# Finishing the last but one projection's second half inside attention, and moving a small norm product to another tile and other PSUM banks

## The chip, the cores and the metric

The kernel runs on one core of a Trainium2 chip. A core has five engines that run side by side[...]: TensorE (PE in the profile, with its weight loads as PEld), VectorE (DVE), ScalarE (ACT), GpSimd (POOL) and SyncE (SP), which in this kernel issues every DMA. The metric is the time of one execution on the device in microseconds (us); a comparison takes the median of several runs. Lower is better.

## The reference, cut to what matters

The input x is 1024 tokens by 512 features. It is normalised, and two branches read it: an attention with 32 query heads and 8 key/value heads of 128 channels, and a feed-forward network with integer weights. The result is x plus the attention's output times a SiLU of the network's output.

```python
xn = layernorm(x)
q = rmsnorm((xn @ Wq.T) per head, q_norm_w)          # 32 heads of 128
k = rmsnorm((xn @ Wk.T) per head, k_norm_w)          # 8 heads
v = (xn @ Wv.T) per head
scores = q @ k.T / sqrt(128) + alibi bias, causal
attn = softmax(scores) @ v
s = attn @ Wo.T
g = silu(down(silu(xn @ gate) * (xn @ up)))          # weights dequantised by groups
out = x + s * g
```

All inputs and the output are float32. The kernel keeps that accuracy by splitting each operand of a product into a high and a low float16 part and adding three products (helper `mm3`, lines 112 to 116).

## The kernel before, in words

**Three stages.** First the feed-forward network (to about 217 us in the profile), then twelve projections (to about 493 us), then attention with the output product (to the end). The order of the instructions of every engine is written out by hand: an engine executes its instructions in the order in which the program issues them.

**The projections.** They are numbered k = 0 to 11 and run in the order kv0, q0, q1, kv1, q2, q3, kv2, q4, q5, kv3, q6, q7 (`projections`, lines 666 to 669). A q projection makes four query heads (512 columns), a kv projection two key heads and two value heads. Number 10 is q6, the last but one, and 11 is q7. Each runs over eight tiles t of 128 tokens (the loop at line 1088). A tile is twelve products of 512 columns into one PSUM bank (`Projection.tile`, line 570). ACT copies the bank to the float32 tile `f` (line 580) and sums its squares per head (line 582); for kv, ACT and DVE also split the values (lines 594 and 595). There are two PSUM rings of two banks for this: even tiles take "m", odd tiles "o". A tile can start when the bank of its ring's last but one user has been read.

**Preparing the next projection's weights.** While projection k runs, `prepare(k + 1, t)` (line 671) is called ahead of tile t. `squares` sums the squares of the weights on ACT (called at t = 6 of the projection before). `norms` (line 514) adds them over the partitions by a small product with ones on PE, and DVE makes a power of two per head from it (`am`, line 526 and those after). `split_head` (line 556) then splits a head's weights into `wh` on ACT (line 561) and `wl` on DVE (line 562), one head per tile. Where the small product lies in PSUM is told by `spare` (line 486): in the "m" ring, so as one more user between two even tiles.

**Finishing a half.** After tiles 3 and 7, `queue_half` (line 767) queues the finishing of four tiles: the inverse root (`inverse` on DVE, `newton` on POOL), and per tile a multiplication on POOL (`normalize`, line 636), a float16 split on DVE (`halves`, lines 648 and 649), a transpose by DMA (`transposed`, line 657) and a store to DRAM (`store`, line 662), each a step or two after the other. Each work is put in a list under the step at which it is due, `finish_step` (line 477) carries out what is due and advances the clock. There are three `f` tiles.

**Attention.** 256 steps n of 128 queries of one head. Eight groups of 32 steps, one per key/value head; a group has four query blocks of 256 tokens, named qb 0 to 3, whose work grows with qb. The first group takes them as 3, 2, 1, 0, later ones as 2, 3, 0, 1. At step n PE makes the scores of n (line 866, PSUM ring "s", two tiles of two banks), DVE adds the bias and takes the row's minimum for n - 1 (line 878), ACT takes the exponential (line 879), ACT and DVE split it into float16 parts (lines 898 and 907), SP transposes it by DMA (line 915), and five steps later PE multiplies by the values (line 930). The first eight steps are run within projections 10 and 11, one after every second tile (lines 1104 to 1106). Queries are written to DRAM per group and read back a block ahead of use; group 6 reads q6, group 7 takes q7 from SBUF.

**The last projection is finished late.** For q7, `queue_half` takes the steps from two tables: `LAST_ROOTS` (the roots of its two halves) and `LAST_PAIRS` (the step of `halves` for each tile). Its steps count from TILES = 96, the number of projection tiles. q6 has been finished at once, its second half within projection 11.

Of the kernel before, what the change touches and what calls it, by code (L numbers as in the profile page):

```python
# [29 lines left out]
NI = FF // P  # L30
# [22 lines left out]
VALUES_STEP = 24  # L53


LAST_ROOTS = {1: 24, 0: 36}
LAST_PAIRS = {4: 46, 5: 78, 6: 110, 7: 142, 2: 174, 3: 221, 0: 224, 1: 229}
LAST_QUERIES = {4: 217, 5: 219, 6: 225, 7: 227, 2: 233, 3: 235, 0: 241, 1: 243}

WO_SPLIT = 6  # L60
# [16 lines left out]
def attention_gated_by_ffn_kernel(ctx, tc, x, gu_w, gu_z, gu_s, dn_w, dn_z, dn_s, wq, wkv, wo, qnw, knw, out):  # L77
# [7 lines left out]
    def ps2(name):  # L85
        return psum[0].tile([P, 2, 512], F32, tag="s", name=name)

    def ps1(tag, name):
        return psum[0].tile([P, 512], F32, tag=tag, name=name)
# [22 lines left out]
    def mm3(ps, lhs, rhs, first, last):  # L112
        (lh, ll), (rh, rl) = lhs, rhs
        te.matmul(ps, lhsT=lh, rhs=rh, start=first, stop=False)  # L114
        te.matmul(ps, lhsT=lh, rhs=rl, start=False, stop=False)  # L115
        te.matmul(ps, lhsT=ll, rhs=rh, start=False, stop=last)  # L116
# [43 lines left out]
    def pair(name):  # L160
        return fpsum.tile([P, 2, 512], F32, tag="pair", name=name)
# [72 lines left out]
    def gu_total(unit, m):  # L234
        a = gu_sums[unit, m, 0]
        ge.tensor_tensor(a, a, gu_sums.pop((unit, m, 2)), ALU.add)
# [11 lines left out]
    def gu_finish(k):  # L248

        if behind[k]:  # L250
            (gu_gate, gu_h)[k](behind[k].pop(0))
# [166 lines left out]
    def dn_load(it):  # L418
        if it % 2 == 0:
            wi = gp.tile([P, 2, DM], I32, tag="wi", name=f"dni{it}", bufs=3)  # L420
            sp.dma_start(wi, dn_w[it * P : (it + 2) * P, :].rearrange("(t p) c -> p t c", p=P))
            dn_raw["pair"] = (wi, wi.bitcast(F32))
        zi = gp.tile([P, DM], I32, tag="dzi", name=f"dnz{it}")
        si = gp.tile([P, DM], F32, tag="dsi", name=f"dns{it}")
        sp.dma_start(zi, dn_z[it].partition_broadcast(P))
        sp.dma_start(si, dn_s[it].partition_broadcast(P))
        dn_raw[it] = tuple(w[:, it % 2, :] for w in dn_raw["pair"]) + (zi, si)

    def dn_dequant(it, engine=ge):
        wi, wf, zi, si = dn_raw[it]  # L430
        ve.tensor_tensor(wf, wi, zi, ALU.subtract)
        engine.tensor_tensor(wf, wf, si, ALU.mult)

    def dn_split_w(it):
        if it % 2 == 0:
            wh = gp.tile([P, 2, DM], F32R, tag="wq", name=f"dnh{it}", bufs=3)
            wl = gp.tile([P, 2, DM], F32R, tag="dwl", name=f"dnl{it}")
            dn_w_hl["pair"] = (wh, wl)
        dn_w_hl[it] = tuple(w[:, it % 2, :] for w in dn_w_hl["pair"])
        split_r(dn_raw.pop(it)[1], *dn_w_hl[it])  # L440

    def dn_split_h(it, tb):
        hh = gp.tile([P, 512], F32R, tag="hh", name=f"hh{it}_{tb}", bufs=3)
        hl = gp.tile([P, 512], F32R, tag="hl", name=f"hl{it}_{tb}", bufs=3)
        split_r(h[:, it, tb * 512 : tb * 512 + 512], hh, hl)
        dn_h_hl[it, tb] = (hh, hl)
# [3 lines left out]
    def wo_squares_load(g):  # L450
        wo_raw[g] = gp.tile([P, NH, DM], F32, tag=("gs", "us")[g % 2], name=f"wo_sq{g}")
        sp.dma_start(wo_raw[g], wo[g * NH * HD : (g + 1) * NH * HD, :].rearrange("(i p) c -> p i c", p=P))

    def wo_squares(g):
        w = wo_raw.pop(g).rearrange("p i c -> p (i c)")
        se.activation(w, w, AF.Square, accum_out=swo[:, g : g + 1])
# [6 lines left out]
    def norm_weights():  # L463
        sp.dma_start(qwb, qnw.partition_broadcast(P))
        sp.dma_start(kwb, knw.partition_broadcast(P))
        ve.tensor_tensor(wn, qwb, kwb, ALU.mult)
        ve.tensor_reduce(wm, wn, AX.X, ALU.max, apply_absolute_value=True)
        ve.tensor_scalar(wm, wm, 1e-5, None, ALU.max)
        for i in range(NH):
            ve.tensor_scalar(cs[:, i : i + 1], wm, STEEPER[i] / (Q_SCALE * Q_SCALE * math.sqrt(HD)), None, ALU.mult)  # L470
        ve.reciprocal(rc, cs[:, NH - 1 : NH])
        ve.reciprocal(wm, wm)
        ve.tensor_scalar(wn, wn, wm, -Q_SCALE, ALU.mult, ALU.mult)
# [10 lines left out]
        finishing.setdefault(clock[0] + steps, []).append(f)  # L484

    def spare(k, name):
        return ps1("m", name) if k else pair(name)[:, 0, :]

    class Projection:
        def __init__(self, k, kind, i):  # L490
# [175 lines left out]
    projections = []  # L666
# [4 lines left out]
    def prepare(k, t):  # L671

        if k < len(projections):
            p = projections[k]
            if t == -1:
                p.squares()
            elif t == 1:
                p.norms()
            elif t == 2:
                p.scale()  # L680
            elif t == 6:
                p.factors()
            if 2 <= t < 2 + p.n:
                p.split_head(t - 2)
            elif p.kind == "kv" and 4 <= t < 6:
                p.split_values(t - 4)

    def down_begin():
        dn_split_w(0)
# [4 lines left out]
    for it in range(3, NI):  # L694
        if it < 3 + 2 * KT:
            projections[(it - 3) // KT].load((it - 3) % KT)
        last = it == NI - 1
        gu_unit(
            it,
            None,  # L700
            it + 1 if not last else None,
            meanwhile={NI - 2: lambda: dn_dequant(0, ve), NI - 1: down_begin}.get(it, lambda: None),
            total=not last,
        )
        if it == NI - 5:
            prepare(0, -1)
        if it == NI - 4:
            prepare(0, 1)
        if it == NI - 3:
            dn_load(0)  # L710
            dn_load(1)
        if last:
            dn_load(2)
            dn_split_h(0, 1)
# [3 lines left out]
    for it in range(NI):  # L718
        for tb in range(2):
            if it == 0:  # L720
                two = [pair(f"dn_ps{tb}_{i}") for i in range(2)]
                acc[tb] = [two[i // 2][:, i % 2, :] for i in range(4)]
            if tb == 0:
                if it + 2 < NI:
                    dn_dequant(it + 2)
                if it + 3 < NI:
                    dn_load(it + 3)
                if it + 1 < NI:
                    dn_split_w(it + 1)
            if it + 1 < NI:  # L730
                dn_split_h(it + 1, tb)
            wh, wl = dn_w_hl[it]
            hh, hl = dn_h_hl.pop((it, tb))
            for i in range(4):
                c = slice(i * P, i * P + P)
                mm3(acc[tb][i], (hh[:, c], hl[:, c]), (wh, wl), it == 0, it == NI - 1)
            if tb:
                if 0 <= it - 3 < HKV:
                    wo_squares_load(it - 3)
                if 0 <= it - 5 < HKV:  # L740
                    wo_squares(it - 5)
                if it in (1, 2):
                    gu_total((NI - 1, None), it - 1)
                elif it == 3:
                    gu_finish(0)
                elif it == 4:
                    gu_finish(1)
                elif it == 5:
                    norm_weights()
                elif NI - 6 <= it < NI - 1:  # L750
                    prepare(0, 8 - NI + it)
                if it == NI - 2:
                    prepare(1, -1)
            if it == NI - 1:
                for i in range(4):
                    go = h[:, i, tb * 512 : tb * 512 + 512]
                    se.activation(go, acc[tb][i], AF.Silu)
                    sp.dma_start(gd[tb * 4 + i], go)
# [8 lines left out]
    def queue_half(p, half):  # L767

        last = p is projections[-1]

        def due(steps, i, f):
            if last and i is None:
                c = TILES + LAST_ROOTS[half]
            elif last:
                c = TILES + LAST_PAIRS[half * HT + i] - 4
            else:
                c = clock[0] + (i or 0)
            finishing.setdefault(c + steps, []).append(f)

        due(0, None, lambda: p.inverse(half))  # L780
        if p.by_root:
            due(1, None, lambda: p.newton(half, True))
        else:
            for i in range(3):
                due((i + 1) // 2, None, lambda i=i: p.newton(half, i == 0))
        for i in range(HT):
            t = half * HT + i
            due(4, i, lambda t=t: p.halves(t))
            due(2, i, lambda t=t: p.normalize(t))
# [221 lines left out]
    late, y_ = [], []  # L1011
    TILES = NT * len(projections)
# [140 lines left out]
```

## Time and profile before

| | us |
|---|---|
| median of 3 runs | 1066.66 (1065.36 to 1067.37) |
| the profiled execution, its own time | 1066.42 |
| its span in the trace | 1064.6 |
| PE busy | 1002.7 (94%) |
| DVE busy | 886.1 (83%) |
| ACT busy | 802.7 (75%) |
| POOL busy | 413.9 (39%) |
| packets of the DMA queue that SP issues to, share of 16 engines' span | 85.4% |

The profile is of one execution. A group of instructions is told by the line of the kernel, the engine and the names of what it writes and reads (out<-in). "Idle before" is the time that the engine stood still ahead of the instruction, and after the arrow stands what ended it. The ends of PE's products are modelled: a product of 512 columns is shown with 0.38 us, while one starts every 0.216 us. So PE is "busy" through short waits, and a loss on PE is best measured from start to start.

### The profile page before, as it was taken

The numbers are of one execution on the slowest core, as the hardware profiler recorded it, in microseconds if no ns is written. First come the engines' busy times: TensorE is split into PE (matmuls) and PEld (weight loads), VectorE is DVE, ScalarE is ACT, GpSimd is POOL, SyncE is SP. The second block draws the span as 40 slices with busy tenths as digits, with TensorE's granted clock in tenths as the row PEclk, the third lists the DMA queues.
The fourth block names the chain that finished last, engine by engine and source line by source line (L and its number), as shares of the span: only waits on it lengthen the run. The fifth ranks groups of instructions, "written<-read, shape, count | busy, mean of one in ns | idle before, by whom it ended". The sixth has DMA issues, their size and how long they took to land.

```text
span 1064.6 us, 18405 instructions
## 1 busy us (share of the span) xinstructions
PE 1002.7 (94%) x5913; PEld 584.6 (55%) x5913; DVE 886.1 (83%) x1745; ACT 802.7 (75%) x2160; POOL 413.9 (39%) x407
## 2 busy tenths in 40 slices
PE   7899899999989999898799999999999999999986
PEld 4344377844444444344566666566666666665563
DVE  7888996638778687788799899898998998979986
ACT  5777644778877787587778788797987888868862
POOL 2588653124545546361343215123141141250732
PEclk9999999999999999999999999999999999999998
DMA  6123259447988989989999999899999998999995
GB/s 202 49 100 119 70 170 302 166 139 162 219 228 188 242 203 235 279 179 207 226 193 214 195 200 222 167 227 197 189 207 193 197 223 182 221 224 194 231 189 129
DMA packets 455039, 204.39 MB, mean 192 GB/s; under 512 B 401506, under 2 KB 411038, under 8 KB 454942
## 3 DMA queue, kind: packets, MB, share of 16 engines
q1 hardware_dynamic: 454942, 203.21, 85.4%
q8 instruction: 46, 0.75, 0.3%
q14 instruction: 51, 0.42, 0.1%
HBM read 77.32 MB, written 27.27 MB: 98 GB/s over the span
## 4 chain that ended last, share of the span: by engine, by line
PE 48%; DVE 17%; ACT 13%; issue 10%; DMA 8%; SPq 2%; POOL 2%; DVEq 0%; ACTq 0%; POOLq 0%
PE gu_ps L267 6%; DMA pT<-p 4%; PE s L114 4%; DVE pf L878 3%; PE s L116 3%; PE s L115 3%; PE op L114 3%; PE op L115 3%; PE av L114 3%; PE op L116 3%; PE av L116 3%; PE av L115 3%; ACT p L898 2%; ACT pf L879 2%; PE ps_q L114 2%
## 5 line engine op out<-in xcount | busy, mean ns | idle before, releaser
L907 DVE SCALAR_TENSOR_TENSOR p<-pf,row,p 128x1024 f16<-128x1024 f32 (+7 forms) x256 | 227.8, 890 | 23.5 <-ACT p L898 20.3
L879 ACT ACTIVATE pf<-pf,row 128x1024 f32<-128x1024 f32 (+7 forms) x256 | 197.6, 772 | 57.2 <-DVE row L878 52.7
L878 DVE CUSTOM_DVE_ANT_0 pf<-s,trel,cs 128x1024 f32<-128x1024 f32 (+7 forms) x256 | 207.2, 809 | 13.7 <-PE s L116 13.4
L898 ACT ACTIVATE p<-pf,row 128x1024 f16<-128x1024 f32 (+7 forms) x256 | 196.5, 768 | 8.4 <-DMA pT<-p 3.5
L114 PE MATMUL av<-pT,vT 128*128 128x256 f16 (+1 forms) x640 | 167.8, 262 | 15.5 <-DMA pT<-p 15.5
L115 PE MATMUL av<-pT,vT 128*128 128x256 f16 (+1 forms) x640 | 167.8, 262 | 0.0
L116 PE MATMUL av<-pT,vT 128*128 128x256 f16 (+1 forms) x640 | 167.6, 262 | 0.0
L114 PE MATMUL s<-kT,qT 128*128 128x512 f16 (+3 forms) x384 | 125.0, 325 | 12.4 <-DVE row L878 12.1
L115 PE MATMUL s<-kT,qT 128*128 128x512 f16 (+3 forms) x384 | 125.0, 326 | 0.0
L116 PE MATMUL s<-kT,qT 128*128 128x512 f16 (+3 forms) x384 | 123.4, 326 | 0.0
L837 POOL TENSOR_SCALAR wor<-wor,rvs 128x512 f32<-128x512 f32 x32 | 54.5, 1702 | 162.8 <-DMA wor<-in_wo 141.5
L114 PE MATMUL ps_q<-wh_q,xth 128*128 128x512 f16 x256 | 97.6, 381 | 2.6 <-DVE am_q L526 2.5
L116 PE MATMUL ps_q<-wh_q,xtl 128*128 128x512 f16 x256 | 97.5, 381 | 0.0
L115 PE MATMUL ps_q<-wl_q,xth 128*128 128x512 f16 x256 | 97.5, 381 | 0.0
L114 PE MATMUL op<-woh,oh 128*128 128x512 f16 x248 | 94.5, 381 | 0.0
L115 PE MATMUL op<-wol,oh 128*128 128x512 f16 x248 | 94.3, 380 | 0.0
L116 PE MATMUL op<-woh,ol 128*128 128x512 f16 x248 | 94.2, 380 | 0.0
L114 PEld LDWEIGHTS <-vT 128*128 128x128 f16 x640 | 62.6, 98 | 56.6 <-DMA pT<-p 9.4
L115 PEld LDWEIGHTS <-vT 128*128 128x128 f16 x640 | 62.6, 98 | 41.3 <-issue 3.5
L941 ACT ACTIVATE oh<-av 128x256 f16<-128x256 f32 x128 | 47.7, 373 | 48.5 <-PE av L116 47.8
L636 POOL TENSOR_TENSOR f_q<-f_q,inv_q 128x512 f32<-128x512 f32 x64 | 77.4, 1237 | 1.1
L844 POOL TENSOR_TENSOR wol<-wor,woh 128x512 f16<-128x512 f32 x32 | 49.4, 1543 | 71.3 <-ACT woh L843 71.3
(194 smaller groups left out, 2255.6 us busy)
## 6 DMA issues: line engine op xcount, KB each, us to landing
qd<-tr_q SPq DMA_DIRECT2D x56, 256.0 KB, 3.4
qT<-qd SPq DMA_DIRECT2D x28, 512.0 KB, 4.5
wq<-in_wq SPq DMA_DIRECT2D x32, 256.0 KB, 3.9
wo_sq<-in_wo SPq DMA_DIRECT2D x8, 1024.0 KB, 9.1
wor<-in_wo SPq DMA_DIRECT2D x32, 256.0 KB, 3.7
gui<-in_gu_w SPq DMA_DIRECT2D x13, 512.0 KB, 3.5
wkv<-in_wkv SPq DMA_DIRECT2D x16, 256.0 KB, 3.8
vd<-v SPq DMA_DIRECT2D x8, 512.0 KB, 4.0
```

The lines of the kernel that those rows point to most:

```text
L114: te.matmul(ps, lhsT=lh, rhs=rh, start=first, stop=False)
L115: te.matmul(ps, lhsT=lh, rhs=rl, start=False, stop=False)
L116: te.matmul(ps, lhsT=ll, rhs=rh, start=False, stop=last)
L267: te.matmul(banks[j][:, k, :], lhsT=w[:, j, ws], rhs=x[:, j, k * 512 : k * 512 + 512], start=x is xth, stop=x is xtl)
L636: ge.tensor_tensor(f, f, ib, ALU.mult)
L837: ge.tensor_scalar(wor[g, i], wor[g, i], rvs[:, g : g + 1], None, ALU.mult)
L844: ge.tensor_tensor(wol[g, i], raw, woh[g, i], ALU.subtract)
L878: ve.tensor_tensor_reduce(p, ps, trel[g][:, S - w :], cs[:, hh : hh + 1], 3e38, ALU.add, ALU.min, least[:, c])
L879: se.activation(p, p, AF.Exp, bias=least[:, c], scale=-1.0, accum_out=total[:, c])
L898: se.activation(p16[u, qt][:, :, 0, :], pf[u, qt], AF.Copy, scale=scale[:, qt : qt + 1])
L907: ve.scalar_tensor_tensor(lo, p, scale, hi, ALU.mult, ALU.subtract)
L941: se.activation(oh, av_ps[u], AF.Copy, scale=1.0 / P_SCALE)
```

## The change

Three edits.

1. The second half of projection 10 (q6, tiles 4 to 7) is no longer finished within projection 11. Its root is due at step 28, its four `halves` at steps 36, 44, 52 and 60; `normalize` is due two steps before, the transpose one step after and the store three steps after each. q7's roots move from steps 24 and 36 to 66 and 70, and its first five `halves` from 46, 78, 110, 142, 174 to 76, 92, 108, 124, 140.
2. `norms` is called ahead of tile 2 instead of tile 1; with it `scale`, `factors`, `split_head` and `split_values` move by one tile. The fourth head's split is thus ahead of tile 6 instead of tile 5. For projection 0, which is prepared within the network, the calls are renumbered and nothing moves.
3. The small product of `norms` takes a tile of the scores' ring "s" for projections 1 to 10, and a bank of the ring "o" for projection 11, where it took one of "m".

```diff
-LAST_ROOTS = {1: 24, 0: 36}
-LAST_PAIRS = {4: 46, 5: 78, 6: 110, 7: 142, 2: 174, 3: 221, 0: 224, 1: 229}
+LAST_ROOTS = {1: 66, 0: 70}
+LAST_PAIRS = {4: 76, 5: 92, 6: 108, 7: 124, 2: 140, 3: 221, 0: 224, 1: 229}
+
+LATE_ROOTS = 28
+LATE_PAIRS = [36, 44, 52, 60]
...
     def spare(k, name):
-        return ps1("m", name) if k else pair(name)[:, 0, :]
+        if k == 0:
+            return pair(name)[:, 0, :]
+        return ps2(name)[:, 0, :] if k < len(projections) - 1 else ps1("o", name)
...
             if t == -1:
                 p.squares()
-            elif t == 1:
+            elif t == 2:
                 p.norms()
-            elif t == 2:
+            elif t == 3:
                 p.scale()
-            elif t == 6:
+            elif t == 7:
                 p.factors()
-            if 2 <= t < 2 + p.n:
-                p.split_head(t - 2)
-            elif p.kind == "kv" and 4 <= t < 6:
-                p.split_values(t - 4)
+            if 3 <= t < 3 + p.n:
+                p.split_head(t - 3)
+            elif p.kind == "kv" and 5 <= t < 7:
+                p.split_values(t - 5)
...
     def queue_half(p, half):
 
         last = p is projections[-1]
+        late = p is projections[-2] and half == 1
 
         def due(steps, i, f):
-            if last and i is None:
+            if late:
+                c = TILES + (LATE_ROOTS if i is None else LATE_PAIRS[i] - 4)
+            elif last and i is None:
                 c = TILES + LAST_ROOTS[half]
```

More of the change, by code (lines that the diff above doesn't have):

```diff
@@ L707, in attention_gated_by_ffn_kernel @@
         if it == NI - 4:
-            prepare(0, 1)
+            prepare(0, 2)
         if it == NI - 3:
@@ L750, in attention_gated_by_ffn_kernel @@
                 elif NI - 6 <= it < NI - 1:
-                    prepare(0, 8 - NI + it)
+                    prepare(0, 9 - NI + it)
                 if it == NI - 2:
```

## The prediction

> **What bounds the kernel now.** I first read the page: PE is busy for 94% of the span, DVE for 83%. So I went to the busy time by stretches (engine busy and number of instructions, granted clock, DMA share, GB/s), cut at the projections' end and at the blocks of attention's second group.
>
> ```profile
> 467.70:493.10 25.40, 24.24 (x120) 11.51 (x119) 20.66 (x32) 19.54 (x79) 11.82 (x17) 1.00 0.96 214
> 493.10:546.40 53.30, 43.85 (x339) 30.24 (x338) 42.82 (x102) 43.30 (x112) 17.84 (x25) 1.00 1.07 219
> 563.00:585.30 22.30, 21.56 (x148) 13.72 (x147) 21.97 (x37) 19.40 (x35) 8.96 (x6) 1.00 1.06 218
> 585.30:601.60 16.30, 15.34 (x125) 11.22 (x123) 12.55 (x35) 12.50 (x37) 5.57 (x7) 1.00 1.12 213
> 615.10:685.50 70.40, 68.38 (x481) 43.95 (x480) 63.15 (x139) 58.10 (x133) 18.51 (x15) 1.00 1.01 198
> ```
>
> PE (first busy column) sets the time almost everywhere: 68.4 of 70.4 us in the third group. It stands still mainly in two places. One is the start of attention, 493 to 546: 9.5 of 53.3 us. The other is inside the projections, where the timeline of PE shows it:
>
> ```profile
> 303.19 0.38 PE L116 MATMUL ps_q<-wh_q,xtl 128*128 128x512 f16 x1
> 305.03 0.17 PE L518 MATMUL n_ps<-sb_q,ones_bf 128*128 128x4 bf16 x1 [1.46 <-DVE v L595]
> ...
> 307.43 0.38 PE L116 MATMUL ps_q<-wh_q,xtl 128*128 128x512 f16 x1
> 309.05 0.38 PE L114 MATMUL ps_q<-wh_q,xth 128*128 128x512 f16 x1 [1.24 <-DVE am_q L526]
> ...
> 440.07 0.16 PE L518 MATMUL n_ps<-sb_q,ones_bf 128*128 128x4 bf16 x1 [2.71 <-DVE v L595]
> ...
> 440.50 0.63 PE L115 MATMUL ps_q<-wl_q,xth 128*128 128x512 f16 x1
> ```
>
> At projection 4's second tile the small product waits until DVE has read kv tile 6 out of the "m" bank it is to take; then tile 2 waits until DVE has read the small product. From start to start, less the pitch of 0.216: 305.03 - 303.19 - 0.22 = 1.62 and 309.05 - 307.43 - 0.22 = 1.40, so 3.03 us. Projection 7 repeats it (371.71 and 375.72, the same 1.46 and 1.24 of idle). At 440.07 (within projection 10) 2.87 us are lost, and the next seven products start every 0.42 instead of 0.216 us: another 1.3.
>
> For the start of attention I took the waits from 485 to 546, and SP's timeline:
>
> ```profile
> PE av L114 <- DMA pT<-p: 5.9, 5, 2.6
> PE s L114 <- DVE row L878: 4.7, 5, 1.8
> ```
>
> ```profile
> 489.49 1.29 SPq L657 DMA_TRANSPOSE tr_q<-q  x1
> 490.87 0.64 SPq L662 DMA_DIRECT2D qd<-tr_q  x1
> 491.60 1.37 SPq L657 DMA_TRANSPOSE tr_q<-q  x1
> 493.06 0.53 SPq L662 DMA_DIRECT2D qd<-tr_q  x1
> 493.65 3.63 SPq L915 DMA_TRANSPOSE pT<-p  x1
> 497.33 0.57 SPq L662 DMA_DIRECT2D qd<-tr_q  x1
> 498.08 1.59 SPq L915 DMA_TRANSPOSE pT<-p  x1
> ```
>
> The probabilities' transpose issued at 493.65 was ready on DVE at 490.15 (start plus length in DVE's timeline): SP was busy with q6's second half. Against DVE's ends, the next ones are issued 3.7, 2.6, 4.3, 5.6 and 6.2 us late, under 1 us only again from 541. In the third group the delay is mostly 0 to 0.8. So here SP and the DMAs behind it are late, and PE's products with the values wait for landings.
>
> **What the Trainium skill says.** "Perfetto Trace Analysis", section on the HWDGE DMA instruction: the shown length is the sequencer generating descriptors, and only at its end is it free for the next instruction; "What DMA-bound means" counts a solid sequencer track as a bound of its own. SP's rows above agree: one starts within 0.1 us of the last one's end. "DMA: Bandwidth & Descriptors", "Issuing engines are not separate DMA queues": all DMAs share 16 engines; the shares of 1.06 to 1.12 agree with crowding. "PSUM — Partial Sum Buffer", "Engine vs sequencer instructions": PE's products start in program order, so tile 1 cannot pass the waiting small product; the trace agrees. "TensorE: Matmul & The Clock Gate", Part 1: an idle window halves the clock; the doubled pitch after 440.07 fits, though the 1.6 us stops show none.
>
> **Part 1, the small product.** Nothing is added: the same 13 products and DVE operations, a tile later. In the "s" ring no bank is in use before step 0, so its wait goes, and even tiles then have both "m" banks. Who is late next? Tile 2 of projection 4 needs kv tile 6's bank: PE would reach it at 303.40 + 2.59 = 306.0, DVE's read ended at 304.97, margin 1.0 us. The fourth `wh` (0.75 us) now comes after kv tile 5's copies on ACT but still ahead of tile 6's, so their end doesn't move. Gain 3.03 twice, and 0.4 at projection 5's product; bound above 6.5, below 4 (if the margin goes half the time). I take 6.0. Cover for the later split: the fourth `wl` is needed only at the next projection, over a tile (2.6 us) later.
>
> Projection 10 differs. The product for 11 is now in "o" behind kv tile 7, read by DVE until 441.41; PE gets there at 437.2 + 2.6 = 439.8 and still waits 1.6, with tile 2 and step 1's scores queued behind it. Then DVE is the limit: it works from 439.6 to 463 with under 2 us idle. The fourth `wl` ended at 461.9; projection 11's first product began at 463.5. A tile later, it comes behind ACT's copies of tile 5 (1.5 us) and `wh` (0.7), at about 462.7. So PE gains 463.5 - 462.7 = 0.8, not 4.2. Bounds 0 and 4.2; I take 1.0.
>
> **Part 2, what leaves projection 11.** DVE loses four pairs (CAST 1.25, 1.26, 0.42, 0.42 and TENSOR_TENSOR 1.41, 0.69 three times: 6.8 us between 478.8 and 487.8) and a root (0.5); POOL 4.7 us and twelve small operations; SP four transposes and four stores (1.30 and 0.52 median: 7.3 us). DVE's scores of step 5 start at 484.4 though PE had them at 473.7. Without the pairs DVE and ACT are 4 to 7 us earlier with steps 5 to 8, and SP is free when they come. PE's loss from 485 to 546, from start to start, is 5.5 on DVE and 6.8 on landings: 12.3 is the bound above. Below: SP's first lateness, 3.5. The landings end PE's waits until 531.5 (slack 0.0 there), so PE gains what the transposes gain, 4 to 7; then SP again issues 16-block transposes of up to 3 us against steps of 2.1. I take 5.5.
>
> **Part 3, what arrives in the second group.** DVE: pairs at 36, 52 and 60 in addition (44 takes 46's place), 0.42 + 0.69 = 1.11 each; less one root (0.52), since q7's go to the third group. The blocks of qb 0 and 1 have 3.7 and 1.4 us of DVE idle for two of them; the first, in a block where DVE is idle 0.6 of 16.6, costs about 0.5. POOL: 1.3 each, covered (its waits there include 19.4 us for `trel`). SP: 1.82 per tile. Adding up SP's rows gives 21.3 us in the 22.3 from 563.0, 13.6 in the next 16.3. Pair 44 adds its transpose and store just there: 23.1 of 22.3. Behind them queue the transposes of the last qb 3 heads, which landed 1.5 and 0.1 us ahead of their products (589.1 and 599.0). So PE is held by about 2. Together 2.5; bound below 0.5 (another landing hides it), above 7.3 (all of SP's time on the path). Pairs 36, 52 and 60 find SP free for 2 to 6 us in their blocks.
>
> **Part 4, later groups.** Two roots enter qb 2 of the third group (1.0 of DVE in 0.3 idle), pairs at 92 and 124 fall into qb 1 with 1.4 idle, the sixth group loses its pair (up to 1.3 of PE's wait for DVE there). I take 0, bounds -1.5 and +1.5.
>
> **Sum.** 6.0 + 1.0 + 5.5 - 2.5 - 0 = 10.0 us. The profiled execution's span is 1064.6 and its own time 1066.42, 1.8 around it and 0.24 under the median. 1066.66 - 10.0 gives 1056.7; I say **1056.5**.
>
> **Rivals.**
> - *The second group gives most of the start back.* SP and the DMA share say that the work only moves from one crowded place to another. With 6 for SP and no gain in projection 10: 6.0 + 5.5 - 6 = 5.5, so 1061. Against it: SP has 8 us free over the other three blocks.
> - *The start is freed wholly.* Early probabilities and an empty SP remove most of the 12.3, and projection 10 gains 3: 6.5 + 3 + 9 - 2 = 16.5, so 1050. Against it: transposes of 3 us per 2.1 us step.
> - *Slower: stores block SP.* Each store of q6 waits on SP, two steps (4.2 us) after its transpose, for that to land. The landing took 3.6 median, 7.5 at most. If all four took 7.5, each would hold SP, and every transpose behind it, for 3.3; with 1.8 of issue, 4 x 5.1 = 20.4 against gains of 12.5: 1074. It decides when a tile costs over 3.1 us on PE's path. For it: nearly all slack at 589 and 599 is gone already. Against: two of the four lie in blocks with spare.
> - *The stops move rather than go.* ACT and DVE, at 18 of 21 us in q projections, become the limit, and PE stops elsewhere: parts 1 and 2 give 2.5, 1066.7. Against it: ACT itself waits 2.2 us for PE right after each stop (at 307.8).
>
> **How the numbers follow.** Chances: my forecast 0.54 (own range 1053 to 1060.5), second group gives back 0.22 (1059 to 1064), wholly freed 0.12 (1047 to 1053), slower by SP 0.07, stops move 0.05. The range from 1051 to 1063.5 takes in nearly all of the first two and a part of the third, 0.8 in all. About 0.2% (2.1 us) is what a measurement of this kernel can tell from no change. Faster: 0.54 + 0.22 + 0.12 = 0.88; within 0.2%: 0.05; slower 0.07.
>
> **What would show it.** Right: no idle ahead of the small product at projections 4 and 7, and none for `am`; at projection 11's first product a wait for `wl`; SP's transposes within 2 us of DVE from 490 to 510; a loss near the second group's qb 3 to qb 0 change behind q6's transposes. Wrong: the small product waiting for the squares instead, PE's stops in the first group unchanged, or a second group over 74 us (it took 68.7, from 546.4 to 615.1).

## The result and the profile after

The changed kernel takes 1072.57 us (median of 6 runs, 1071.88 to 1074.61) against 1067.70 for the kernel before (6 runs, 1065.36 to 1069.83): a ratio of 1.0049, interval 1.0032 to 1.0066. It is slower; 1056.5 was forecast. The profiled execution took 1072.69, its span is 1070.8, against 1064.6; these two lie 6.2 apart, the medians 4.9. Cut at ACT's copy of a projection's first tile and at DVE's first operation on the scores of a group, the spans differ like this (us):

| stretch | before | after | difference | forecast |
|---|---|---|---|---|
| network, to projection 0's first tile | 220.8 | 221.4 | +0.6 | 0 |
| projections 0 to 10 | 246.9 | 250.9 | +4.0 | -7.0 |
| projection 11 and first group | 78.7 | 72.8 | -5.9 | -5.5 |
| second group | 68.7 | 74.6 | +5.9 | +2.5 |
| third group | 70.4 | 72.8 | +2.4 | 0 |
| the rest | 379.1 | 378.4 | -0.7 | 0 |

One of the three large terms came out as forecast, the first group's. PE's waits in the projections, 223 to 493 us, in the changed kernel (line that waited, for whom, us in total, times, longest):

```profile
PE ps_q L117 <- ACT wh_q L566: 5.9, 3, 2.6
PE ps_q L118 <- DVE wl_q L567: 3.7, 3, 1.3
```

In the kernel before, the same stretch held these:

```profile
PE n_ps L518 <- DVE v L595: 5.6, 3, 2.7
PE ps_q L114 <- DVE am_q L526: 2.5, 2, 1.2
PE s L114 <- DVE row L878: 1.2, 2, 0.8
PE n_ps L518 <- ACT jk_q L582: 0.3, 1, 0.3
PE ps_kv L114 <- DVE v L595: 0.3, 1, 0.3
```

The waits at the small product are all gone, as forecast, and 9.6 us of waiting stand at another place where there were 9.9. The new place is the first tile of projections 4, 7 and 10. PE's timeline after, at projection 4:

```profile
302.51 0.38 PE L117 MATMUL ps_q<-wh_q,xth 128*128 128x512 f16 x1 [1.43 <-ACT wh_q L566]
304.14 0.59 PE L118 MATMUL ps_q<-wl_q,xth 128*128 128x512 f16 x1 [1.25 <-DVE wl_q L567]
304.51 0.63 PE L119 MATMUL ps_q<-wh_q,xtl 128*128 128x512 f16 x1
304.94 0.63 PE L117 MATMUL ps_q<-wh_q,xth 128*128 128x512 f16 x1
...
307.34 0.38 PE L117 MATMUL ps_q<-wh_q,xth 128*128 128x512 f16 x1
```

PE reaches the q projection and finds the fourth head's `wh`, then its `wl`, not made. Behind the pair the products start every 0.43 us instead of 0.216 (half clock), seven or eight times: about 1.5 us more. In projections 3 to 10 there are 22 such products after and 7 before, those all behind the stop at 440.07. The two waits within projection 4 of before, twelve products apart, had none behind them. From start to start, less the pitch, PE loses 15.2 us in projections 4 to 10, against 11.7 before, which is most of the 4.0.

The start of attention, PE's waits from 485 to 545 and SP's timeline:

```profile
PE av L117 <- DMA pT<-p: 3.7, 4, 2.3
PE s L117 <- DVE row L886: 2.1, 2, 1.8
```

```profile
488.03 8.92 SPq L923 DMA_TRANSPOSE pT<-p  x3
497.00 1.06 SPq L842 DMA_DIRECT2D wor<-in_wo  x1
498.90 2.00 SPq L923 DMA_TRANSPOSE pT<-p  x1
```

q6's transposes and stores are gone from between those of the probabilities. From 490 to 520 the probabilities' transposes are now issued 0 to 4.3 us behind DVE; before, they were up to 6.5 us late. PE's waits fell from 10.6 to 5.8 us.

The stretches after that answer to those shown of before: the first group behind projection 11, then qb 3 and qb 0 of the second group, the whole second group (68.7 us before) and the third:

```profile
493.80:545.10 51.30, 45.46 (x353) 31.59 (x351) 42.78 (x103) 43.05 (x112) 18.53 (x26) 1.00 1.02 205
562.10:584.20 22.10, 21.62 (x148) 13.77 (x147) 22.07 (x38) 19.55 (x35) 7.98 (x5) 1.00 1.13 217
584.20:605.40 21.20, 17.09 (x125) 11.91 (x124) 13.73 (x38) 12.54 (x37) 7.61 (x10) 0.92 1.08 211
545.10:619.70 74.60, 69.59 (x466) 43.12 (x464) 65.27 (x145) 56.77 (x130) 17.80 (x16) 0.98 1.03 203
619.70:692.50 72.80, 69.29 (x481) 44.11 (x480) 65.92 (x148) 57.96 (x133) 27.57 (x40) 1.00 1.01 196
```

Nearly the whole loss of the second group lies in its block qb 0, the third row: 21.2 us against 16.3. No engine is full in it. SP's timeline shows who is late:

```profile
577.51 3.02 SPq L923 DMA_TRANSPOSE pT<-p  x1
580.58 1.30 SPq L662 DMA_TRANSPOSE tr_q<-q  x1
581.99 1.64 SPq L923 DMA_TRANSPOSE pT<-p  x1
583.67 1.14 SPq L842 DMA_DIRECT2D wor<-in_wo  x1
584.90 3.00 SPq L923 DMA_TRANSPOSE pT<-p  x1
588.00 0.53 SPq L667 DMA_DIRECT2D qd<-tr_q  x1
588.63 5.38 SPq L923 DMA_TRANSPOSE pT<-p  x2
```

SP has no pause. Tile 44's transpose at 580.58 and its store at 588.00 stand in the row, and the probabilities that DVE ended at 581.6, 584.3, 586.8 and 589.4 are issued 3.3, 4.4, 3.5 and 5.6 us later. In the kernel before, the four in these places were 0.1, 0.6, 0.0 and 0.6 late. From issue to landing these and their neighbours take 4.1 to 5.5 us in both kernels, where the trace shows a landing, so it is the issue that is late, not the transfer that is slower. PE waits for these landings at 589.42, 595.96 and 602.72, 4.6 us in all from start to start less the pitch, and behind the second wait its products start at half the pace until 600.5 (granted clock of the block 0.92).

### The profile page after: what moved, and what is told of

The parts are those of the page before. It is cut to its first block, busy times and chain, and to the rows that moved or that the text cites. A ratio compares the mean times of both kernels' runs of the same rounds, so it can differ in the third digit from the quotient of the medians.

```text
span 1070.8 us, 18379 instructions
## 1 busy us (share of the span) xinstructions
PE 1008.7 (94%) x5913; PEld 587.2 (55%) x5913; DVE 885.5 (83%) x1745; ACT 801.9 (75%) x2160; POOL 404.4 (38%) x407
## 4 chain that ended last, share of the span: by engine, by line
PE 40%; DVE 23%; ACT 14%; issue 11%; DMA 9%; POOL 1%; SPq 1%; DVEq 0%; ACTq 0%; POOLq 0%
DVE pf L886 6%; DMA pT<-p 6%; PE gu_ps L270 6%; DVE p L915 5%; PE ps_q L118 3%; ACT pf L887 3%; PE ps_q L119 3%; ACT p L906 3%; PE ps_q L117 3%; PE av L117 2%; ACT jk_q L587 2%; PE s L117 2%; PE op L118 2%; PE op L119 2%; PE op L117 2%
## 5 line engine op out<-in xcount | busy, mean ns | idle before, releaser
L641 POOL TENSOR_TENSOR f_q<-f_q,inv_q 128x512 f32<-128x512 f32 x64 | 75.7, 1206 | 1.0
```

Source lines behind the costliest of these rows:

```text
L641: ge.tensor_tensor(f, f, ib, ALU.mult)
```

## The experiments

Each was compared with runs of the kernel before on its own chip; the medians of these lie between 1067.2 and 1068.2, so two rows are best compared by their ratios. "P0-10" are projections 0 to 10, "P3-9" the seven projections 3 to 9, "start" is projection 11 and the first group, g2 and g3 are the second and third group; these come from each one's profiled execution, which can lie a few us off the median beside it. The diffs show the main lines of an edit only.

| kernel | us | ratio, interval | P0-10 | P3-9 | start | g2 | g3 |
|---|---|---|---|---|---|---|---|
| before | 1067.70 | 1 | 246.9 | 159.0 | 78.7 | 68.7 | 70.4 |
| the change | 1072.57 | 1.0049 (1.0032 to 1.0066) | 250.9 | 162.3 | 72.8 | 74.6 | 72.8 |
| 1 small product only | 1072.88 | 1.0046 (1.0031 to 1.0062) | 251.0 | 162.4 | 78.6 | 70.4 | 71.4 |
| 2 finishing only | 1072.24 | 1.0041 (1.0028 to 1.0054) | 247.4 | 159.6 | 74.1 | 74.9 | 72.9 |
| 3 banks only | 1067.22 | 0.9995 (0.9979 to 1.0010) | 246.2 | 158.7 | 78.4 | 68.6 | 70.6 |
| 4 later, in "m" | 1076.55 | 1.0069 (1.0045 to 1.0093) | 251.3 | 162.4 | 78.7 | 69.7 | 71.5 |
| 5 four `f` | 1067.22 | 0.9993 (0.9981 to 1.0005) | 247.0 | 157.1 | 79.5 | 69.1 | 70.7 |
| 6 change, four `f` | 1072.99 | 1.0050 (1.0033 to 1.0067) | 249.8 | 159.3 | 72.6 | 74.8 | 72.9 |
| 7 stores held | 1066.63 | 0.9993 (0.9978 to 1.0009) | 248.3 | 160.4 | 75.2 | 70.0 | 75.7 |
| 8 spread, four `f` | 1063.36 | 0.9953 (0.9937 to 0.9969) | 249.1 | 159.0 | 72.8 | 68.2 | 70.5 |
| 9 change, split no later | 1072.34 | 1.0041 (1.0025 to 1.0058) | 248.0 | 160.0 | 72.9 | 73.9 | 73.6 |
| 10 all mended | 1066.05 | 0.9976 (0.9962 to 0.9989) | 251.0 | 160.9 | 73.0 | 68.3 | 70.7 |
| 11 spread only | 1061.82 | 0.9950 (0.9933 to 0.9968) | 247.0 | 159.2 | 74.4 | 67.7 | 70.6 |
| 12 squares later | 1080.11 | 1.0103 (1.0081 to 1.0125) | 257.4 | 163.9 | 78.7 | 69.1 | 70.7 |
| 13 change, squares later | 1074.24 | 1.0058 (1.0041 to 1.0074) | 249.3 | 159.3 | 75.0 | 74.5 | 72.9 |
| 14 spread, squares later | 1074.52 | 1.0056 (1.0036 to 1.0076) | 255.3 | 162.0 | 73.9 | 68.2 | 70.8 |
| 15 the same, small product later | 1065.67 | 0.9979 (0.9968 to 0.9990) | 249.3 | 159.3 | 73.0 | 67.3 | 70.6 |
| 16 late split alone | 1070.24 | 1.0020 (1.0010 to 1.0030) | 248.7 | 159.8 | 77.9 | 68.8 | 71.0 |
| 17 late product alone | 1073.58 | 1.0055 (1.0036 to 1.0073) | 251.0 | 163.2 | 79.4 | 69.5 | 71.3 |

### Which edit costs what (1 to 4)

**1, the small product only**: the change with the tables and `queue_half` of the kernel before.

```diff
-LAST_ROOTS = {1: 66, 0: 70}
-LAST_PAIRS = {4: 76, 5: 92, 6: 108, 7: 124, 2: 140, 3: 221, 0: 224, 1: 229}
+LAST_ROOTS = {1: 24, 0: 36}
+LAST_PAIRS = {4: 46, 5: 78, 6: 110, 7: 142, 2: 174, 3: 221, 0: 224, 1: 229}
```

> Only the small product's edit (a tile later, in the scores' banks, weights' split a tile later); q6 and q7 are finished as before. Theory A (the later split puts the fourth head's wh and wl on PE's path at the start of projections 4, 7 and 10, since ACT runs behind PE in kv projections): the projections take 4 us longer than before, attention is as before, so +4 (+3 to +6), and PE waits for wh (L561) and wl (L562) there. Theory B (the projections' loss comes from the moved finishing of q6, not from this edit): -6, no such wait.

**2, the finishing only**: the kernel before with the change's tables and `queue_half`, `prepare` and `spare` untouched.

> Only the moved finishing of q6's second half and of q7; the small product as before. Theory A: projections 0 to 10 as before with PE's stops at 305, 309, 372, 376 and 440 unchanged; the start of attention 5.8 us shorter, the second group 5.9 and the third 2.4 us longer: +2.5 in all (0 to +5). Theory B: the second group's loss came with a disturbed start from the projections, and without it stays under 2.5: -3 or better.

Each edit alone makes the kernel slower. The small product's part costs 4 us in P0-10 and leaves the start as it was; the finishing's part leaves P0-10 alone, gains 4.6 at the start and loses 6.2 in the second and 2.5 in the third group. So the second group's loss is not an echo of the projections. In the execution shown, the small product alone also lengthens the second group by 1.7 and the third by 1.0, and the two ratios do not add up (0.46% and 0.41% alone, 0.49% together); the reason for neither was looked for.

**3, the banks only**: the small product and the splits at their old tiles, but in the scores' ring.

```diff
-        return ps1("m", name) if k else pair(name)[:, 0, :]
+        if k == 0:
+            return pair(name)[:, 0, :]
+        return ps2(name)[:, 0, :] if k < len(projections) - 1 else ps1("m", name)
```

> The small product stays ahead of tile 1, and so does the whole split of the weights; only its place changes: the scores' ring for projections 1 to 10, m as before for 11. Finishing as before. Theory A (the bank was the cause of the stops, the lateness of the loss): the stops at projections 4, 5 and 7 go, nothing new appears: -6 (-4 to -6.5). Theory C (ACT and DVE are the limit, and PE stops elsewhere whatever the bank): within 1 us of before, with waits for wh and wl at the next tiles.

**4, later, in "m"**: the other half, every call of `prepare` a tile later as in the change, the bank as before.

> The small product and the split a tile later, as in the change, but in the m ring as before; finishing as before. Theory A: the waits for wh and wl at projections 4, 7 and 10 are there as in the change (+4), and its bank may add to it: +4 to +8. Theory D (the place in the scores' ring or in o makes the new waits): no wait for wh or wl, -3 to +1.

The banks alone do what they were to do: the stop of 3.03 us within projection 4 is gone. PE's timeline of 3, and ACT's copy of projection 4's first tile:

```profile
303.42 0.38 PE L116 MATMUL ps_q<-wh_q,xtl 128*128 128x512 f16 x1
303.81 0.16 PE L520 MATMUL n_ps<-sb_q,ones_bf 128*128 128x4 bf16 x1
...
306.21 0.38 PE L116 MATMUL ps_q<-wh_q,xtl 128*128 128x512 f16 x1
306.43 0.38 PE L114 MATMUL ps_q<-wh_q,xth 128*128 128x512 f16 x1
```

```profile
308.13 0.59 ACT L582 COPY f_q<-ps_q 128x512 f32<-128x512 f32 x1 [2.25 <-DVE q L651]
```

And nothing is won: the time is that of its own kernel before (1067.22 and 1067.15), projections 3 and 6 take 24.3 us each as before, and PE waits elsewhere, in projections 5, 7 and 8 and at two places of 10. Seen from PE's own starts, projections 4 to 9 gain 1.8 us, and projection 10 gives 1.5 of them back. The tile later costs by itself, in "m" too: 251.3, in an execution that was the fastest of its six.

### The second group: SP or DVE (7)

**7, stores held**: as 2, with DVE's and POOL's work at the same steps, but SP's transposes at steps 57, 59, 61 and 63 and the stores two steps later, in the group's last block.

```diff
-                defer(1, lambda: self.transposed(t, a16))
+                held = self.k == len(projections) - 2 and t >= HT
+                defer(TILES + LATE_STORES[t - HT] - clock[0] if held else 1, lambda: self.transposed(t, a16))
```

> The first part of the change alone (the late finishing, with the small product as in the kernel before), with one thing altered: DVE's and GpSimd's work on the four tiles stays at steps 36, 44, 52 and 60, but SyncE's transposes of them and the stores are held until steps 57, 59, 61 and 63 (stores two steps later). The part alone took 74.9 us for the second group of 32 steps, against 68.7 before. Theory S (the added transposes and stores stand ahead of the transposes of `p` on SyncE and make TensorE wait for `pT`): the second group takes 70 to 72 us and the time is 1068 to 1070. Theory V (the vector engine is full in those steps, and what is added to it there costs its own duration): the second group still takes 74 to 75 us, 1071 to 1073.

The second group with its qb 0 block, first of 2, then of 7:

```profile
542.70:617.60 74.90, 67.93 (x466) 42.26 (x465) 65.27 (x145) 56.84 (x130) 20.86 (x16) 1.00 1.02 203
582.30:603.30 21.00, 15.36 (x124) 11.00 (x122) 13.23 (x38) 12.49 (x37) 9.26 (x9) 1.00 1.06 212
```

```profile
543.50:613.60 70.10, 67.97 (x467) 42.44 (x466) 65.17 (x145) 56.81 (x130) 19.25 (x16) 1.00 0.99 200
582.60:599.20 16.60, 15.38 (x125) 11.18 (x123) 13.55 (x37) 12.59 (x37) 7.60 (x10) 1.00 1.12 211
```

DVE's busy time (third busy column) is the same, 65.2 us, and the group is 4.8 us shorter; PE's waits for landings in it, 5.6 us in 2, are not there in 7. So the loss of qb 0 is SP's row and not DVE's fullness. Theory S holds, and the ratio falls from 1.0041 to 0.9993, about 5 us, a little more than expected. What is left, 1.3 us in the second group, stands in the blocks of pairs 36 and 60 (0.5 and 0.8); to the first of them 7 adds nothing on SP. The held work is not free: in the profiled execution the last transposes collide with the probabilities of the third group's start (75.7 us for that group). That execution took 1070.82; 11 of the 14 took 1064.7 to 1067.9.

### A place where it costs less (8, 11, 10)

**8, spread, four `f`**: the kernel before with q6's second half finished only in qb 0 blocks of groups 2 to 4, transposes in the block after, q7's tiles also in qb 0 blocks, and a fourth `f` buffer. **11, spread only**: without that buffer.

```diff
-LAST_ROOTS = {1: 24, 0: 36}
-LAST_PAIRS = {4: 46, 5: 78, 6: 110, 7: 142, 2: 174, 3: 221, 0: 224, 1: 229}
+LAST_ROOTS = {1: 112, 0: 144}
+LAST_PAIRS = {4: 118, 5: 146, 6: 150, 7: 178, 2: 182, 3: 221, 0: 224, 1: 229}
+LATE_ROOTS = 48
+LATE_PAIRS = [54, 82, 86, 114]
+LATE_STORES = [58, 90, 93, 122]
```

> The kernel before with a fourth buffer for `f`, and the finishing of the last but one projection's second half put only into the blocks whose scores are narrowest (first two query tiles), where DVE is busy 12.5 us of 16 to 17: its root at step 48, its tiles at 54, 82, 86 and 114, with transposes held to the block after; the last projection's finishing follows at 112, 118, 144, 146, 150, 178 and 182, again in such blocks, and leaves the places of before (46, 78, 110, 142, 174), where DVE is busy over 95%. Theories V and C together: the start of attention gains 4 to 6 us as in the change, the second group stays at 68 to 70 us and each of the next four is up to 1 us shorter, and the projections gain what the fourth buffer alone gains: 1052 to 1058. If in those blocks it is TensorE's wait for `pT` that counts (SyncE is busy 13.6 us of 16.3 there), the groups lose 1 to 2 us each: 1060 to 1064.

> The kernel that spread the finishing over the narrow blocks, without the fourth `f` buffer. The buffer alone moved the time by less than 0.1%, so the spread should be what gained: 1061 to 1065. If the gain needed the buffer: 1066 to 1068.

Both beat the kernel before. 11 does by 0.5% and is the fastest of all. It keeps most of the start's gain (74.4 against 78.7) and the second group does not pay for it: 67.7 us. For 8 a gain in the projections had been added that the buffer did not bring, so the time missed its first range; it lies in the second, but not for the reason given there, as the second group took 68.2.

**10, all mended**: 8 with the change's small product and the split of 9 below.

> The changed kernel with that earlier split, and with the finishing of both projections placed as in the kernel that spread it over the narrow blocks (tiles at 54, 82, 86, 114 and 118, 146, 150, 178, 182, transposes held to the block after, a fourth buffer for `f`), which took 1063.4 us with the small product and the split of before. Theory H: the gain in the projections, 2 to 4 us against before, adds to it: 1058 to 1062. Theory C: 1063 to 1068.

1066.05 us, 2.7 above 8 (the intervals of the two just overlap): the later small product seems to cost here too, though no row of half-clock products is left in P3-9.

### What the projections are held by (5, 6, 9, 12 to 17)

**5, four `f`**, and **6, the change with four `f`**: `bufs=3` becomes 4 for the tag "f" (lines 573 and 960).

> The kernel before with a fourth buffer for the projections' `f` tiles (and so for the gates' tiles, which share the tag); nothing else is changed, and no instruction is added or moved. Theory C (a projection of keys and values is set by a chain of ACT and DVE: ACT's copy of tile 4, and of the next projection's tile 0, waits for the `f` buffer which DVE's halves of the projection before it free; TensorE's stops at the small product are slack of that chain): the waits of the copy on DVE (2.28 us in the 4th projection of before) go, the 4th, 7th and 10th projection fall from 24.3, 24.3 and 26.4 us to 21.5 to 23 and the time to 1059 to 1063. Rival D (the stops on the small product set the pace, and the copy's waits only follow from them): projections as before, 1065 to 1069.

> The changed kernel with a fourth buffer for the `f` tiles. Theory C: with the chain loosened ACT and DVE run ahead, so that the later split of the weights no longer comes too late; the stops on `wh` and `wl` of 1.4 to 2.7 us at the 5th, 8th and 11th projection's first tile fall below 1 us each, the projections take 4 us or more less than in the change (1.0 us or more less at each of the three) and the time is 1063 to 1067. Rival D (the split is a tile later by program order, and no buffer helps): the stops stay at 1.4 us or more, 1070 to 1074.

Half of theory C came true. ACT's wait for `f` at tile 4 went: from a kv projection's first to its fifth tile it now takes 9.7 us instead of 11.2 in the kernel before, and about 9 instead of 12.9 in the change. Yet projections 4 and 7 took 1.5 to 2.2 us longer and projection 10 about 2, and the time of neither kernel fell. In 6 the stops on `wh` and `wl` stayed, as rival D said. So the wait for `f` is not all that holds the projections; what takes its place in 5 was not followed further.

**9, the change, split no later**: the last head's split as early as before.

```diff
-            if 3 <= t < 3 + p.n:
-                p.split_head(t - 3)
-            elif p.kind == "kv" and 5 <= t < 7:
+            for i in range(p.n):
+                if t == (3, 4, 4, 5)[i]:
+                    p.split_head(i)
+            if p.kind == "kv" and 5 <= t < 7:
```

> The changed kernel, with one thing altered: the four parts of a query projection's weights are split at tiles 3, 4, 4 and 5 of the projection before, not at 3, 4, 5 and 6, so that the last part is as early as in the kernel before. Theory H (the later split puts the wait on `wh` of 1.6 to 2.7 us and that on `wl` of 1.4 us next to each other at the first tile of the 5th, 8th and 11th projection, and after such a pair TensorE runs 7 or 8 products at half clock, 1.45 us each time; that, not the length of the stops alone, is the projections' loss): the two waits fall below 1 us together, at most 8 half-clock products are left in the seven projections from the 4th to the 10th (22 in the change, 5 before), these seven take 155 to 158 us (162.3 in the change, 159.0 before), and the time is 1065 to 1068. Theory C (a chain of ACT and DVE sets the pace, so that work put earlier only delays their other work): 161 to 163 us for the seven and 1071 to 1074 in all.

Neither theory fits. The pair of waits shrank to 0.44 us at projection 4, but at 7 and 10 the wait on `wh` of 2.6 us stayed; P3-9 fell to 160.0, the median did not follow. Run 4 has 8 half-clock products in projections 3 to 10, run 17 below none and the change 22, and P3-9 takes 162.4, 163.2 and 162.3 us: half clock is not what sets the length, for where it is gone PE waits longer.

**12 to 15, squares later**: the squares of projection k + 1's weights at tile 0 of projection k, not at tile 6 of k - 1; in the kernel before, in the change, in 11, and in 11 with the change's small product.

```diff
-            prepare(k + 1, t)
-            if t == NT - 2:
-                prepare(k + 2, -1)
+            if t == 0 and k > 0:
+                prepare(k + 1, -1)
+            prepare(k + 1, t)
```

> The kernel before, with the squares of a projection's weights (3.2 us of ACT) issued at the first tile of the projection before it, not at the last tile but one of the projection before that; the small product stays at the second tile. Theory Q (the chain through ACT's squares sets a projection of keys and values): ACT does them while it would wait for `f` (2.25 us at 305.5 in the trace of before); the seven projections from the 4th to the 10th take 153 to 157 us against 159.0, the time is 1061 to 1065. Rival P (the stops at the small product set the pace; they now wait for later squares): 159 to 163 us for the seven, 1067 to 1071.

> The changed kernel with the squares at the first tile of the following projection, two tiles ahead of its small product. Theory Q: the seven projections fall from 162.3 to 154 to 158 us and the time from 1072.6 to 1065 to 1069; the loss that stays is the second and third group's. Rival P: 161 to 164 us for the seven, 1071 to 1074.

> The kernel that spread the finishing over the narrow blocks (1061.8 us) with the squares at the first tile of the following projection; the small product as before. Theory Q: 1055 to 1059. Rival P: 1062 to 1066.

> The same with the change's small product, a tile later and in the scores' banks. If the later product costs only because the chain is tight (theory Q), it now costs nothing or gains up to 2 us against the run with the product as before: 1053 to 1059. If it costs by itself: 3 to 5 us more than that run.

None of the four came out as expected. With the old small product PE now waits for the squares in nearly every projection, and 12 and 14 lose 11 to 13 us against their like. With the later small product P3-9 falls by 3.0 (13), but the rest takes it back. Only here is the tile later worth something: 15 is 8.9 us under 14, and still 3 to 4 over 11.

**16 and 17** do one half each of what moves with the small product: 16 is 3 with the query weights' split at tiles 3 to 6; 17 is 1 with it at 2 to 5.

```diff
-            if 2 <= t < 2 + p.n:
-                p.split_head(t - 2)
+            s = 3 if p.kind == "q" else 2
+            if s <= t < s + p.n:
+                p.split_head(t - s)
```

> The kernel with the small product at its old tile in the scores' banks (1067.2 us, the seven projections from the 4th to the 10th 158.7 us), with the query weights split at tiles 3 to 6 of the projection before, not at 2 to 5; keys and values as before. If the late split is what costs (its last part then meets TensorE at the first tile of the 5th, 8th and 11th projection): waits on `wh` and `wl` there of 3 us or more together, 161 to 163 us for the seven, 1070 to 1073. If the later product is: 157 to 160 for the seven, 1066 to 1068.5.

> The change's small product alone (a tile later and in the scores' banks, old finishing: 1072.9 us, 162.4 us for the seven projections), with the query weights split at tiles 2 to 5, the first part straight behind the small product. If the late split is what costs: 157 to 160 us for the seven, 1065 to 1069. If the later product is (ACT then waits for the factors ahead of the first part): 161 to 164 us, 1070 to 1075.

The later product costs all 4 us (P0-10 251.0, 1073.58). The later split by itself costs about half of that (248.7; ratio 1.0020 against 0.9995 for 3), at the first tiles forecast for it, though the waits there come to 2.2 us at projections 4 and 7 where 3 or more was expected. They do not add up either: 17 costs as much as 1. As I read it, both hold the same chain.

That chain can be read in the traces. ACT's copies of projection 3's fifth tile and of projection 4's first, in the kernel before and in the change (the idle time and its releaser in brackets):

```profile
294.72 0.37 ACT L580 COPY f_kv<-ps_kv 128x256 f32<-128x256 f32 x1 [2.28 <-DVE q L649]
...
307.83 0.59 ACT L580 COPY f_q<-ps_q 128x512 f32<-128x512 f32 x1 [2.25 <-PE ps_q L116]
```

```profile
297.18 0.37 ACT L585 COPY f_kv<-ps_kv 128x256 f32<-128x256 f32 x1 [4.27 <-DVE q L654]
...
309.93 0.59 ACT L585 COPY f_q<-ps_q 128x512 f32<-128x512 f32 x1 [2.24 <-DVE q L654]
```

The copy of tile 4, and that of the next projection's tile 0, take an `f` buffer that DVE's `halves` of q1 has to read first. The trace of before puts the second wait down to PE; but tile 0's last product had ended at 303.57, DVE's L649 ended at 307.72, 0.11 ahead of the copy, and in the change and in 3 DVE is named. DVE's rows of before:

```profile
286.29 0.15 DVE L526 TENSOR_SCALAR am_q<-n_ps 128x4 f32<-128x4 f32 x1
...
293.20 1.41 DVE L649 TENSOR_TENSOR q<-f_q,q 128x512 f16<-128x512 f32 x1
294.54 1.52 DVE L562 SCALAR_TENSOR_TENSOR wl_q<-wq,am_q,wh_q 128x512 f16<-128x512 f32 x1
...
307.03 0.69 DVE L649 TENSOR_TENSOR q<-f_q,q 128x512 f16<-128x512 f32 x1
```

From the first tile's copy to the fifth's it takes 11.2 us in projections 3, 6 and 9 of the kernel before, of 2 and of 3, 10.9 in 16, 12.9 in the change, in 1, 4 and 9, and 13.9 in 17. So every kernel with three `f` buffers and the small product a tile later has about 1.7 us or more on top here, three times over; in the change the rest of those projections gives 0.4 back in each of the first two and 1.8 in the third. That is 2.8 of the 4.0 us; the others come in steps of 0.6 and less, mainly in projections 2 and 10.

DVE's timeline of the change, ahead of the copy at 297.18, says why:

```profile
289.97 0.10 DVE L531 TENSOR_SCALAR am_q<-n_ps 128x4 f32<-128x4 f32 x1
...
290.72 0.16 DVE L536 TENSOR_TENSOR eps<-eps,steep 128x4 f32<-128x4 f32 x1
290.80 0.42 DVE L600 TENSOR_TENSOR v<-ps_kv,v 128x256 f16<-128x256 f32 x1
291.14 0.42 DVE L653 CAST q<-f_q 128x512 f16<-128x512 f32 x1
291.59 1.41 DVE L654 TENSOR_TENSOR q<-f_q,q 128x512 f16<-128x512 f32 x1
292.92 1.52 DVE L567 SCALAR_TENSOR_TENSOR wl_q<-wq,am_q,wh_q 128x512 f16<-128x512 f32 x1
```

In the kernel before, the five small operations that make `am` ran from 286.3 to 287.2, and DVE then still waited for ACT's values. A tile later they stand in a stretch without a pause from 288.4 to 298.0, ahead of the L654 that frees `f` (295.66 to 297.07). So one more L654 and one more L567 ahead of it slip into the time in which POOL normalises q1's tiles (291.3 to 296.5), where they take 1.41 and 1.52 us instead of 0.69 and 0.74; before, of these two operations only the L649 that frees `f` itself, and the L562 behind it, lay there. With 0.83 for the five operations, less 0.58 for a `wl` that moved behind, that adds up to 1.75, the whole of the 1.7 us. The sum is read off the traces; no run changed DVE's order alone. With a fourth buffer (6) this wait is gone, but the late split still holds PE at the first tile of projections 4, 7 and 10, by 1.3 to 2.6 us and 1.4 more. So what stays open is how much of the loss each of the two is worth where both are present; and no run took away both the stop at the small product (3) and the wait for `f` (5).

## Why the prediction was wrong

**Part 1 failed, and with it the sign.** "Its wait goes" was right, at projections 4 and 7 and for `am`. The first failed step is "Gain 3.03 twice": run 3 takes the stop away and wins nothing. By the traces PE's stop was slack beside the chain of ACT and DVE through `f`, where ACT's wait at 307.83 is put down to PE and is DVE's. That very wait was used against the rival that "the stops move rather than go" (0.05), which is what happened; run 3 shows it without any later tile. The rival's own time, 1066.7, lacked the price of the later tile. The second failed step is "Cover for the later split: the fourth `wl` is needed only at the next projection, over a tile (2.6 us) later". PE had reached that projection at 301.1, while ACT made the fourth `wh` from 301.71 and DVE the `wl` from 303.39. Tiles on PE are no clock for ACT and DVE: ACT copied tile 5 at 300.70, when PE started the last product of tile 7. The third is "Nothing is added": the same operations, a tile later, cost 4 us (runs 1, 4 and 17). Forecast -7.0, measured +4.0; with -7.0 there, and all else as measured, the change would have been about 5 us faster.

**Projection 10.** A wait for `wl` was looked for at projection 11's first product. There is none there; it stands at the first tile of 4, 7 and 10. Of the gain of 1.0 nothing came: projections 9 and 10 together take 0.6 us longer.

**Part 2 held.** -5.5 forecast, -5.9 measured, and by its mechanism: SP free of q6's work, landings earlier. The other kernels without that work in projection 11 gained 3.5 to 6.1 there; that it came so near is in part luck. The sign named for it, transposes within 2 us of DVE from 490 to 510, held to 502 only; then they were up to 3.3 late.

**Part 3 had the right place and too small a size.** The loss lies at the change from qb 3 to qb 0, behind tile 44's transpose and store, as said, and run 7 shows SP to be the cause. The term "So PE is held by about 2" measured 4.6 us of waits for landings and about 1.7 us at half clock after them. It was summed as if SP's 1.8 us too many were paid once; but SP stayed 3.3 to 5.6 us late over eight transposes, each late one followed at once by the next. 5.9 is inside the bounds of 0.5 and 7.3, and the sign of being wrong, "a second group over 74 us", came true with 74.6. For SP, "Pairs 36, 52 and 60 find SP free" was not seen to be wrong; but the blocks of 36 and 60 are 0.5 and 0.8 longer.

**Part 4** was put at 0 with a bound of 1.5; the third group lost 2.4, 1.7 of it in the block with the roots, where DVE is busy for 17.8 of 18.2 us, and 0.8 in that of pair 92 (13.0 of 14.3 us). Pairs 60 and 124, in blocks qb 1 too, cost the same 0.8 each; the 1.4 us of idle that was to hide them did not.

**The rivals.** "Slower: stores block SP" gave 1074, near the time measured, but its mechanism, landings of 7.5 us holding each store, is not what happened: the store at 588.00 followed straight on the row before it, and of the four only the one at 605.53 held SP, for 0.6 us.

## What to carry to other kernels

A stop of the busiest engine is worth its length only if nothing else sets the same pace; take it away in thought and ask which buffer the other engines would wait for next, above all where two of them hand tiles round a ring of three. Check the releaser that a trace names against the time at which that engine was done. Before moving work out of one crowded stretch, add up the issuing queue as well as the engines in the stretch it goes to, and put it where both have room: the same finishing cost 6 us in one place and nothing measurable in another. A small operation that is free where its engine waits anyway costs its length where the engine has no pause: the five for `am` were free before and cost 0.83 us a tile later.

## What was unexpected of the hardware

In these traces DVE's operations on 128x512 take about twice their time while POOL multiplies: L654 a median of 1.41 us (9 cases over 80% covered by L641 between 220 and 493 us) against 0.69 (39 cases apart from it), the CAST L653 1.11 (0.92 to 1.27) against 0.42, L567 1.52 in three of four cases against 0.75. The Trainium skill, "GPSIMD Engine Reference", section "Key points", says that the two engines share their SBUF interfaces and that DVE instructions with two SBUF inputs, or in a two-port mode, contend there. L654 and L567 read two such inputs, and their rows agree; the CAST reads one, and no run here shows its mode.

In the change, the two waits at the first tile of projections 4, 7 and 10 (1.43, 2.57 and 1.88 us of idle for `wh`, one product, 1.25 for `wl`) were followed by half-clock products each time, two waits of 1.46 and 1.24 with twelve products between them (305.03 and 309.05 before) by none. The length of the waits does not decide it alone: the same pair of 2.12 and 1.15 to 1.26 us in 13 had 12, 0 and 7 half-clock products behind it at the three places, and 0.82 and 1.25 in 4 had 0, 0 and 8. The Trainium skill, "TensorE: Matmul & The Clock Gate", Part 1, puts the idle window that lowers the clock at about 3.4 us; the pairs of the change lose 3.0, 4.1 and 3.5 us from start to start, but in 13 all three lose 3.7. What decides it is not shown here.
